# A four-layer network on one core: the scan's product with B queued ahead of other VectorE steps, and small matmuls in column quarters

## The chip, the cores and the metric

One core of one Trainium2 chip. The metric is device time in microseconds (us) of one launch. Engines: PE (TensorE), PEld (its weight loads), DVE (VectorE), ACT (ScalarE), POOL (GpSimd), SP (SyncE, which issues DMAs).

## The reference

Four images x of 96 channels by 64 x 64 pixels go through four layers, each with a residual.

```
x = x + ssm(group_norm(x))          # layer 0: norm, projection, 3x3 conv, selective scans in
                                    # 4 directions, norm, gate z, projection
x = x + deform(group_norm(x))       # layer 1: offsets, mask = 3x3 conv; bilinear samples; conv
t = tokens(x)
t = t + fft_mix(layer_norm(t)); t = t + ffn_fp8(layer_norm(t))          # layer 2
t = t + linear_attn(layer_norm(t)); t = t + ffn_fp8(layer_norm(t))      # layer 3
```

The selective scan, for each of 4 images, 4 directions, 192 channels d and 16 states n, over 4096 positions:

```
h[t] = exp(delta[t] * A[d,n]) * h[t-1] + (delta[t] * u[t]) * B[n,t]
y[t] = sum over n of h[t] * C[n,t]
```

A layer norm needs, at each position, the mean over channels of the squared centred values (the variance).

## The kernel before, in words

**The scan.** Layer 0's scan is cut into 1536 units (`Unit`): 8 channels x 16 states on the 128 partitions, 1024 positions in a row. A unit passes five engines. `fetch` (ACT's DMA queue) brings delta, copied to all states, as `da`; `decay` (L895, ACT) makes exp(delta A) of it; `inflow` (L901, PE) spreads delta u over the partitions into `db`, a PSUM tile with two buffers; `recur` multiplies db by B in place (L915, DVE) and runs the recurrence over da and db (L918, DVE) into `hh`; `weigh` (L925, L927, POOL) multiplies hh by C; `total` (L946, PE) folds the states of two units into `py`, with 32 output columns a product, in four column groups of the array; `settle` and `store` bring the sum out. B and C come with `fetch_step`, delta u with `fetch_block` on SP's queue, six units ahead for `fetch_block`.

`scan` writes out the order by hand. In iteration n it issues, if due, `fetch_step` and `fetch_block`, then inflow(n+1), decay(n+2), total(n-5, n-4) in odd iterations, one fetch, recur(n) with product and recurrence together, weigh(n-2), settle, store, and yields.

**Everything else** runs beside it in two streams of Python generators, joined in `layers23`: `ends` (layer 0's `before` for images 0 to 3, then layers 2 and 3 of each image) and `middle` (`behind`, layer 0's output norm and projection, and layer 1 of each image). An image can be sampled only when its scans are done, and layers 2 and 3 of an image wait for its layer 1. After each unit, the streams put in steps until the planner says stop. Nothing waits at run time for the plan: the plan fixes the order of each engine's instructions, and `in_program_order` keeps it.

**The planner.** `Clock` keeps for each engine the planned end of what is queued. A step names its work as costs in us (`cost(pe=.., dve=..)`); `has_room` lets it in if each engine it uses is planned to end no later than now plus AHEAD (3, 3, 5, 7 us). "Now" is VectorE's planned end or `due`, whichever is later, and `due` grows by PACE (4.8 us) a unit. BESIDE (6 us) bounds the VectorE work beside one unit. `pipe` runs the chains of one stage, a few at a time; tags in `takes` and `frees` count buffers. Outside pipelines (group norm statistics, the steps of `inv_sqrt_steps`, `positions`) a step goes through `Stream.step` alone.

**Norm.** `centred` does one layer norm's first part, in 8 chunks of 512 positions: a product with the centring matrix (L457, PE, "lnc"), square and copy (L462, L463, ACT), and a product of the squares with a matrix whose only non-zero column is number j (L468, PE, "lnv"), so that chunk j's variance lands in row j of one accumulator. Then 1/sqrt, and `spread` (L483) brings row j back to all partitions with a one-hot column of the identity. It is called in `normed_rows` (layer 0) and `normed` (layers 2 and 3). `behind` has its own such norm over 192 channels (L1022, "va"), two chunks at a time.

**Offsets.** `offsets` (layer 1) convolves the padded image with 27 filters, padded to 96 columns: 9 products a chunk, all into the same PSUM rows (L1149, "po"). ScalarE adds the bias (L1159, "oc"), PE transposes the pixels (L1165, "pt") and the offsets (L1170, "pm"), ScalarE copies both, and SP issues 8 stores of the pixels per chunk into a table in DRAM (L1178), from which the samples are gathered (L1251, POOL's queue). Samples are weighted at L1260 (DVE) and transposed at L1277 (PE). The other VectorE step named below is L752 (softplus in layer 0's `steps`).

Of the kernel before, what the change touches and what calls it, by code (L numbers as in the profile page):

```python
# [25 lines left out]
CH = 512  # L26
# [18 lines left out]
def prepare(x, **w):  # L45
# [66 lines left out]
    a["wom"] = wide(om.transpose(1, 2, 0), 96)  # L112
# [87 lines left out]
PACE = 4.8  # L200


class Clock:
# [4 lines left out]
    def __init__(self):  # L208
        self.ends = [0.0] * 4

        self.own = 0.0


        self.idle, self.beside = 0.0, 0.0

        self.due = 0.0

# [8 lines left out]
    def has_room(self, work, ready):  # L226
        now = self.now()
        idle = self.idle if self.own is None else self.own
        if self.own is None and work[DVE] and self.beside >= BESIDE:
            return False  # L230
        first = next((e for e in (PE, ACT, DVE, POOL) if work[e]), None)
        if ready > (now if first is None else max(self.ends[first], idle)):
            return False
        return all(not w or e <= now + a for w, e, a in zip(work, self.ends, AHEAD))

# [25 lines left out]
def pipe(net, chains, width, every=0, **tiles):  # L261
# [5 lines left out]
    while True:  # L267
# [9 lines left out]
        for n, chain in enumerate(active):  # L277
# [4 lines left out]
            if not all(free[tag] for tag in chain.takes):  # L282
                continue
# [5 lines left out]
        for tag in chain.takes:  # L289
            free[tag] -= 1  # L290
        step = next(chain.steps, None)
# [41 lines left out]
class Net:  # L333
# [3 lines left out]
    def __init__(self, ctx, tc, ins):  # L337
# [5 lines left out]
        for name in ("vecs", "ident", "cen96", "grp3"):  # L343
# [3 lines left out]
        for n in (C, DI):  # L347
            t = self.to_row[n] = self.const.tile([128, 135], F32, name=f"to_row{n}")
            nc.vector.memset(t, 0.0)
            nc.vector.memset(t[:, 7:8], 1.0 / n)  # L350
# [96 lines left out]
    def centred(self, x, cen, dst, key, pool, bias=None):  # L447
# [4 lines left out]
        self.hold(1)  # L452

        def chain(j):
            cs = slice(j * CH, (j + 1) * CH)
# [3 lines left out]
            sq = pool.tile([C, CH], F32, name=f"lnq{key}_{j}", tag="lnq", bufs=2)  # L459
# [4 lines left out]
            else:  # L464
                nc.scalar.activation(sq, pc, AF.Square, bias=bias)
                nc.scalar.activation(d, view(pc), AF.Identity, bias=bias)
            yield cost(pe=1.1, act=1.2)
            nc.tensor.matmul(  # L468
                var, lhsT=self.to_row[C][:C, 7 - j : 135 - j], rhs=sq, start=(j == 0), stop=(j == NCH - 1)
            )  # L470
            yield cost(pe=1.0)

        yield from pipe(self, (chain(j) for j in range(NCH)), 2)
# [36 lines left out]
class Layer0:  # L510
# [95 lines left out]
    def normed_rows(self, b, x, pad, rows, as_rows):  # L606
# [3 lines left out]
        with tc.tile_pool(name=f"l0n{b}", bufs=2) as sm:  # L610
# [21 lines left out]
            def chain(j):  # L632
                pb = net.spread(rs, j, C, f"0_{b}")
# [152 lines left out]
    def scan(self):  # L786
# [23 lines left out]
        for n in range(len(units) + 7):  # L810
# [3 lines left out]
            if n == 0:  # L814
# [5 lines left out]
                self.inflow(at(0))  # L820

# [20 lines left out]
            clock.unit(self.scanned[1])  # L842
            yield True

# [64 lines left out]

    def recur(self, u, free):  # L910

        nc, clock = self.net.nc, self.net.clock
        clock.add(DVE, 1.22, u.spread)
        self.scanned = (self.scanned[1], clock.add(DVE, 2.33, max(u.decayed, free)))
        nc.vector.tensor_mul(u.db, u.db, u.bc[:, 0, :])  # L915
# [52 lines left out]
    def behind(self, b):  # L968
# [6 lines left out]
        with (  # L975
# [4 lines left out]
            for j0 in range(NCH - HB, -1, -HB):  # L980
# [18 lines left out]
                def centred(i):  # L999
# [12 lines left out]
                    for g, (o, c0, n) in enumerate(((ca, 0, 128), (cc, 128, D2))):  # L1012
# [24 lines left out]
                def gated(i):  # L1037
# [6 lines left out]
                    pb = net.spread(rstd, i, 128, key)  # L1044
# [26 lines left out]
class Layer1:  # L1071
# [41 lines left out]
    def offsets(self, b, om):  # L1113
# [3 lines left out]
        with tc.tile_pool(name=f"l1a{b}", bufs=1, side="right") as pre:  # L1117
# [26 lines left out]
            def chunk(j):  # L1144
                r0 = j * NR
                po = net.mm(f"po{b}_{j}", 96)
                for k in range(9):
                    dy, dx = divmod(k, 3)
                    nc.tensor.matmul(  # L1149
                        po,  # L1150
                        lhsT=wom[:, k, :],
                        rhs=pad[:, r0 + dy : r0 + dy + NR, dx : dx + W],
                        start=(k == 0),
                        stop=(k == 8),
                    )
# [13 lines left out]
                for q in range(4):  # L1169
                    nc.tensor.transpose(pm[:, q, :], oc[:, 128 * q : 128 * q + 128], net.ident[:27, :27])  # L1170
# [293 lines left out]
def normed(net, t, tl, key, pool):  # L1464
# [6 lines left out]
    def chain(j):  # L1471
        cs = slice(j * CH, (j + 1) * CH)
        pb = net.spread(rs, j, C, key)
# [251 lines left out]
```

## Time and profile before

| | us |
|---|---|
| median of three runs | 9105.8 (9103.93 to 9124.99) |
| the profiled execution | 9119.14 |
| its span, first to last instruction | 9117.0 |
| first scan starts / last scan ends | 368.2 / 7990.6 |
| VectorE busy / GpSimd / PE / ScalarE | 6993.7 / 6374.1 / 6752.4 / 4179.8 |
| mean granted PE clock | 0.818 of full speed |

A row of instructions in the profile reads: line, engine, operation, names out<-in, shape, count, then busy time in us and mean ns of one, then the engine's idle time just before them and what ended most of it. A row of the timeline reads: start, duration (us), engine, line, operation, names, shapes, count of merged instructions, and in brackets the idle time before with its releaser. An fp32 matmul shows as two records. The page's slices, a fortieth of the span each (tenths of busy time):

```profile
DVE  0367877887898898878898989889899988836514
POOL 0486679766789998787799977666799966627701
PEclk8676977798777899777888987789888878886597
```

The dense stretches of POOL (slices 12 to 15, 20 to 22, 29 to 31) are the gathers of images 0, 1 and 2; those of image 3 lie in slices 36 and 37, after the scan.

### The profile page before, as it was taken

The page shows a single profiled execution, that of the slowest core. Times are in us where ns is not written, and L with a number is a line of the kernel's source. Part 1 is how long each engine was busy: PE and PEld are TensorE (multiplying, and loading weights), DVE is VectorE, ACT ScalarE, POOL GpSimd, SP SyncE. Part 2 cuts the span into 40 slices and gives each one's busy share as a digit, 9 for nine tenths or more (in the row PEclk, how much of TensorE's full clock was granted, in tenths as well). Part 3 has the DMA queues.
Part 4 walks back from the last instruction along what each step waited for, and adds up shares of the span by engine and source line. Part 5 has one row for each costly group of instructions (what it writes and reads, how often), then busy time and mean ns, then how long its engine had stood idle before and what let it go on. Part 6 is the DMA issues. An engine that isn't in the chain of part 4 may idle for free.

```text
span 9117.0 us, 93017 instructions
## 1 busy us (share of the span) xinstructions
PE 6752.4 (74%) x31832; PEld 3066.5 (34%) x31832; DVE 6993.7 (77%) x4932; ACT 4179.8 (46%) x5798; POOL 6374.1 (70%) x4755
## 2 busy tenths in 40 slices
PE   6664967697866679676788877788777768885497
PEld 2111311132222234211245542244433435433283
DVE  0367877887898898878898989889899988836514
ACT  4574667565554445566533335543343344431123
POOL 0486679766789998787799977666799966627701
PEclk8676977798777899777888987789888878886597
DMA  1466777777877887787888876677777777824410
GB/s 50 127 184 170 186 194 213 202 185 180 210 208 210 218 211 207 201 210 192 213 209 218 212 189 173 172 189 188 210 197 197 197 166 190 190 59 139 130 52 12
DMA packets 775821, 1609.05 MB, mean 176 GB/s; under 512 B 247665, under 2 KB 338829, under 8 KB 773238
## 3 DMA queue, kind: packets, MB, share of 16 engines
q10 hardware_dynamic: 244224, 843.17, 36.7%
q1 hardware_dynamic: 457398, 533.38, 21.7%
q0 software_dynamic: 73728, 226.57, 9.3%
q8 instruction: 253, 4.15, 0.2%
q14 instruction: 218, 1.79, 0.1%
HBM read 1346.50 MB, written 256.29 MB: 176 GB/s over the span
## 4 chain that ended last, share of the span: by engine, by line
PE 34%; DVE 21%; POOL 16%; DMA 13%; issue 9%; ACT 5%; SPq 1%; ACTq 0%; DVEq 0%; POOLq 0%
DVE hh L918 9%; POOL hh L927 7%; DVE db L915 5%; PE pc L662 5%; POOL g L1251 4%; PE py L946 4%; PE f L1371 3%; PE db L901 3%; PE ps L1277 3%; PE po L1149 2%; DVE g L1260 2%; DMA da<-de 2%; DMA du<-du 2%; PE pd L1293 2%; DMA g<-table,idx 1%
## 5 line engine op out<-in xcount | busy, mean ns | idle before, releaser
L927 POOL TENSOR_TENSOR hh<-hh,bc 128x1024 f32<-128x1024 f32 x1536 | 3665.5, 2388 | 350.0 <-DVE hh L918 234.6
L918 DVE TENSOR_TENSOR_SCAN hh<-da,st,db 128x1024 f32<-128x1024 f32 x1152 | 2703.5, 2347 | 217.0 <-PE py L946 67.3
L915 DVE TENSOR_TENSOR db<-db,bc 128x1024 f32<-128x1024 f32 x1536 | 1868.7, 1217 | 409.8 <-PE db L901 398.1
L895 ACT ACTIVATE da<-da,w_al 128x1024 f32<-128x1024 f32 x1536 | 1742.4, 1148 | 742.0 <-DMA da<-de 300.5
L901 PE MATMUL db<-du,rep 96*128 96x512 bf16 x3072 | 1072.3, 437 | 802.5 <-DVE hh L918 733.0
L1251 POOL DMA_INDIRECT g<-table,idx x1152 | 1340.3, 1163 | 397.7 <-issue 230.8
L946 PE MATMUL py<-hh,w_fold 128*32 128x512 f32 x6144 | 1094.7, 734 | 103.3 <-POOL hh L927 77.6
L918 DVE TENSOR_TENSOR_SCAN hh<-da,db 128x1024 f32<-128x1024 f32 x384 | 877.9, 2286 | 62.1 <-PE py L946 8.8
L1277 PE MATMUL ps<-w_ident,g 128*96 128x128 f32 x3744 | 603.3, 320 | 385.7 <-issue 250.1
L901 PEld LDWEIGHTS <-rep 96*128 96x128 bf16 x3072 | 275.2, 105 | 1736.2 <-issue 1153.0
L1260 DVE TENSOR_TENSOR g<-g,wt 128x1152 f32<-128x1152 f32 x384 | 701.8, 1828 | 163.9 <-DMA g<-table,idx 158.7
L1285 ACT COPY st<-ps 96x384 f32<-96x384 f32 x384 | 182.0, 474 | 1233.0 <-PE ps L1277 1085.0
L925 POOL COPY st<-hh 128x1 f32<-128x1 f32 x1152 | 280.3, 243 | 654.7 <-DVE hh L918 601.9
L1277 PEld LDWEIGHTS ps<-w_ident,g 128*96 128x96 f32 x3744 | 493.7, 148 | 616.6 <-issue 369.2
L749 POOL TENSOR_TENSOR w<-w,ex 128x512 f32<-128x512 f32 x192 | 245.7, 1280 | 525.4 <-ACT w L746 519.4
L662 PE MATMUL pc<-pad,wc 96*128 96x512 f32 x1152 | 533.6, 610 | 45.7 <-DMA wc<-wc_d 42.1
L752 DVE SCALAR_TENSOR_TENSOR rl<-pd,lw 128x512 f32<-128x512 f32 x192 | 130.9, 682 | 475.0 <-POOL lw L750 461.2
L771 PE MATMUL pr<-ex,w_ident 128*128 128x512 f32 x384 | 287.2, 838 | 158.8 <-POOL ex L761 79.5
L946 PEld LDWEIGHTS py<-hh,w_fold 128*32 128x32 f32 x6144 | 162.7, 120 | 633.2 <-issue 391.2
L1517 POOL CAST xqf<-fl 96x512 fp8e5<-96x512 f32 x64 | 46.8, 738 | 454.5 <-DVE fl L1475 407.4
L662 PEld LDWEIGHTS pc<-pad,wc 96*128 96x128 f32 x1152 | 219.1, 195 | 325.1 <-issue 309.7
L1293 PE MATMUL pd<-st,wdc 96*128 96x256 f32 x1152 | 315.1, 426 | 4.2 <-ACT st L1285 3.1
(249 smaller groups left out, 9519.0 us busy)
## 6 DMA issues: line engine op xcount, KB each, us to landing
da<-de ACTq DMA_DIRECT2D x1536, 512.0 KB
du<-du SPq DMA_DIRECT2D x512, 192.0 KB
bc<-bcd SPq DMA_DIRECT2D x128, 512.0 KB
du<-du SPq DMA_DIRECT2D x128, 384.0 KB
y<-yb SPq DMA_DIRECT2D x384, 128.0 KB
de<-rl SPq DMA_DIRECT2D x128, 256.0 KB
m<-in_dft SPq DMA_DIRECT2D x128, 256.0 KB
ad<-y ACTq DMA_DIRECT2D x192, 128.0 KB
```

Of the source, the lines that this page charges most:

```text
L662: nc.tensor.matmul(pp, lhsT=wc[:, q, g * 128 : (g + 1) * 128], rhs=pad[:, r0 + dy : r0 + dy + NR, dx : dx + W], start=(q == 0), stop=(q == 8),
L771: nc.tensor.matmul(pr, lhsT=net.ident, rhs=ex, start=True, stop=False)
L895: self.net.nc.scalar.activation(u.da, u.da, AF.Exp, scale=self.al[:, a : a + 1])
L901: self.net.nc.tensor.matmul(db[:, h, :], lhsT=self.rep[:96, u.s % 4, :], rhs=u.du[u.s // 4][:, h * CH : (h + 1) * CH], start=True, stop=True,)
L915: nc.vector.tensor_mul(u.db, u.db, u.bc[:, 0, :])
L918: nc.vector.tensor_tensor_scan(u.along(u.hh), u.along(u.da), u.along(u.db), first, ALU.mult, ALU.add)
L927: self.net.nc.gpsimd.tensor_mul(u.hh, u.hh, u.bc[:, 1, :])
L946: nc.tensor.matmul(py[p0 : p0 + 32], lhsT=self.fold[:, u.i, :], rhs=hc[:, h * CH : (h + 1) * CH], start=u.sums["add"] is None and u.i == 0 ...
L1251: nc.gpsimd.indirect_dma_start(out=g[:, k, :], out_offset=None, in_=self.tables[b % 2], in_offset=bass.IndirectOffsetOnAxis(ap=idx[:, n : ...
L1260: nc.vector.tensor_mul(g4, g4, w4.unsqueeze(2).to_broadcast([128, 12, C]))
L1277: nc.tensor.matmul(pt[:, k, :], lhsT=g[:, k, c * C : (c + 1) * C], rhs=net.ident, is_transpose=True, start=(c == 0), stop=(c == corners - 1),)
L1293: nc.tensor.matmul(po, lhsT=wdc[:, k, :], rhs=st[:, k, :], start=(k == 0), stop=(k == 8))
```

## The change

1. The product of unit n+1 with B leaves `recur` for a method of its own, `enter`. After unit n has been issued it is pending. `pipe` calls `precede` ahead of each step it issues: if that step has VectorE work and db of unit n+1 is planned to be there MARGIN (0.5 us) before VectorE's planned end, the product is issued ahead of the step. What is still pending when the streams are done is issued then, ahead of the next unit.
2. PACE goes from 4.8 to 4.7.
3. The offsets' convolution writes product k to rows 32 (k mod 4) onward, with filters padded to 32 columns; the bias is added over all 128 rows (only rows 0 to 26 have one), and the transposes of the offsets become products with a matrix `add4`, which sums the four quarters on the way.
4. The variances: a chunk writes its own quarter of the columns (32 wide), and four chunks' products are issued together in a chain `sums`; square buffers go from two to four and are counted by a tag. Chunk j's variance lands in row 32 (j mod 4) + j div 4. In `behind` the two chunks write halves (64 columns).

```diff
-    a["wom"] = wide(om.transpose(1, 2, 0), 96)
+    a["wom"] = wide(om.transpose(1, 2, 0), 32)
+    a["add4"] = (np.arange(128)[:, None] % 32 == np.arange(27)[None]).astype(f)
...
-PACE = 4.8
+MARGIN = 0.5
+PACE = 4.7
...
+    def precede(self, work):
+        if self.enter and work[DVE] and self.own is None and self.entered + MARGIN <= self.ends[DVE]:
+            self.enter()
...
@@ pipe
-            if not all(free[tag] for tag in chain.takes):
+            if not all(free[tag] > 0 for tag in chain.takes):
...
+        clock.precede(known.get((chain.kind, chain.done), (0.0,) * 4))
         step = next(chain.steps, None)
...
@@ Net.__init__
-            t = self.to_row[n] = self.const.tile([128, 135], F32, name=f"to_row{n}")
+            t = self.to_row[n] = self.const.tile([128, 65], F32, name=f"to_row{n}")
...
-            nc.vector.memset(t[:, 7:8], 1.0 / n)
+            nc.vector.memset(t[:, 1:2], 1.0 / n)
...
@@ Net.centred
+            yield wait(new=True, takes="sq")
...
-            sq = pool.tile([C, CH], F32, name=f"lnq{key}_{j}", tag="lnq", bufs=2)
+            sq = sqs[j] = pool.tile([C, CH], F32, name=f"lnq{key}_{j}", tag="lnq", bufs=4)
...
-            yield cost(pe=1.1, act=1.2)
-            nc.tensor.matmul(
-                var, lhsT=self.to_row[C][:C, 7 - j : 135 - j], rhs=sq, start=(j == 0), stop=(j == NCH - 1)
-            )
-            yield cost(pe=1.0)
-
-        yield from pipe(self, (chain(j) for j in range(NCH)), 2)
+            yield cost(pe=1.1, act=1.2, frees=f"v{j // 4}")
+
+        def sums(r):
+            yield wait(takes=f"v{r}")
+            for q in range(4):
+                nc.tensor.matmul(
+                    var[32 * q : 32 * q + 32],
+                    lhsT=self.to_row[C][:C, 1 - r : 33 - r],
+                    rhs=sqs[4 * r + q],
+                    start=(r == 0),
+                    stop=(r == 1),
+                )
+            yield cost(pe=1.3, frees="sq sq sq sq")
+
+        def chains():
+            for r in range(2):
+                for q in range(4):
+                    yield chain(4 * r + q)
+                yield sums(r)
+
+        yield from pipe(self, chains(), 5, every=-99, sq=4, v0=-3, v1=-3)
...
@@ normed_rows and normed
-                pb = net.spread(rs, j, C, f"0_{b}")
+                pb = net.spread(rs, 32 * (j % 4) + j // 4, C, f"0_{b}")
...
@@ scan: before the first unit, and after each unit
+                self.next = at(0)
+                self.enter()
...
+            self.next = at(n + 1)
+            if self.next is not None:
+                clock.enter, clock.entered = self.enter, self.next.spread
             yield True
+            if clock.enter:
+                self.enter()
...
+    def enter(self):
+        u, clock = self.next, self.net.clock
+        clock.enter = None
+        clock.add(DVE, 1.22, u.spread)
+        self.net.nc.vector.tensor_mul(u.db, u.db, u.bc[:, 0, :])
+
     def recur(self, u, free):
         nc, clock = self.net.nc, self.net.clock
-        clock.add(DVE, 1.22, u.spread)
         self.scanned = (self.scanned[1], clock.add(DVE, 2.33, max(u.decayed, free)))
-        nc.vector.tensor_mul(u.db, u.db, u.bc[:, 0, :])
...
@@ behind
-                            var,
-                            lhsT=net.to_row[DI][:n, 7 - i : 135 - i],
+                            var[64 * i : 64 * i + 64],
+                            lhsT=net.to_row[DI][:n, 1:65],
                             rhs=sq,
-                            start=(i == 0 and g == 0),
-                            stop=(i == HB - 1 and g == 1),
+                            start=(g == 0),
+                            stop=(g == 1),
...
@@ offsets
-                po = net.mm(f"po{b}_{j}", 96)
+                po = net.mm(f"po{b}_{j}")
                 for k in range(9):
                     dy, dx = divmod(k, 3)
+                    p0 = 32 * (k % 4)
                     nc.tensor.matmul(
-                        po,
+                        po[p0 : p0 + 32],
...
-                        start=(k == 0),
-                        stop=(k == 8),
+                        start=(k < 4),
+                        stop=(k >= 5),
                     )
-                    if k in (2, 5):
-                        yield cost(pe=2.6, holds=1, takes="oc" if k == 5 else "")
-                oc = pre.tile([27, CH], F32, name=f"oc{b}_{j}", tag="oc")
-                nc.scalar.activation(oc, po[:27], AF.Identity, bias=net.vec(V_OMB, 27))
-                yield cost(pe=2.6, act=0.7, new=True, takes="pix")
+                yield cost(pe=3.0, holds=1, takes="oc")
+                oc = pre.tile([128, CH], F32, name=f"oc{b}_{j}", tag="oc")
+                nc.scalar.activation(oc, po, AF.Identity, bias=net.vec(V_OMB))
+                yield cost(act=0.7, new=True, takes="pix")
...
-                    nc.tensor.transpose(pm[:, q, :], oc[:, 128 * q : 128 * q + 128], net.ident[:27, :27])
+                    nc.tensor.matmul(
+                        pm[:, q, :], lhsT=oc[:, 128 * q : 128 * q + 128], rhs=net.add4, start=True, stop=True
+                    )
```

More of the change, by code (lines that the diff above doesn't have):

```diff
@@ L216, in __init__ @@
         self.due = 0.0
+        self.enter, self.entered = None, 0.0
     def now(self):
@@ L342, in __init__ @@
         self.psum = ctx.enter_context(tc.tile_pool(name="mm", bufs=3, space=PSUM))
-        for name in ("vecs", "ident", "cen96", "grp3"):
+        for name in ("vecs", "ident", "cen96", "grp3", "add4"):
             setattr(self, name, self.load(name, self.const))
@@ L452, in centred @@
         self.hold(1)
+        sqs = {}
         def chain(j):
+            yield wait(new=True, takes="sq")
             cs = slice(j * CH, (j + 1) * CH)
@@ L1043, in gated @@
                     nc.sync.dma_start(zc, self.z_d[b][128:, cs])
-                    pb = net.spread(rstd, i, 128, key)
+                    pb = net.spread(rstd, 64 * i, 128, key)
                     yield cost(pe=1.2, holds=1)
@@ L1472, in chain @@
         cs = slice(j * CH, (j + 1) * CH)
-        pb = net.spread(rs, j, C, key)
+        pb = net.spread(rs, 32 * (j % 4) + j // 4, C, key)
         yield cost(pe=1.2, holds=1)
```

## The prediction

> **What bounds the kernel now.** I read the stage sums first, then the groups, then single stretches of the timeline.
>
> The stretch sums (columns: window, length, then busy time and instructions of PE, PEld, DVE, ACT, POOL, then clock, DMA share, GB/s), cut at the first and the last scan:
>
> ```profile
> 0.00:368.00 368.00, 224.99 (x452) 87.51 (x453) 25.80 (x52) 163.81 (x203) 39.11 (x38) 0.79 0.23 64
> 368.00:7991.00 7623.00, 5738.65 (x27140) 2483.21 (x27140) 6489.29 (x4229) 3733.61 (x5028) 5899.10 (x4342) 0.83 0.76 196
> 7991.00:9117.00 1126.00, 788.80 (x4241) 495.82 (x4240) 478.58 (x652) 282.36 (x567) 435.93 (x376) 0.77 0.29 79
> ```
>
> The scan stage is 7623 of 9117 us, and VectorE is its fullest engine: 6489/7623 = 85%, POOL 77%, PE 75%. The groups show what VectorE does there (busy, mean ns | idle before, releaser):
>
> ```profile
> L918 DVE TENSOR_TENSOR_SCAN hh<-da,st,db 128x1024 f32<-128x1024 f32 x1152 | 2703.5, 2347 | 217.0 <-PE py L946 67.3
> L915 DVE TENSOR_TENSOR db<-db,bc 128x1024 f32<-128x1024 f32 x1536 | 1868.7, 1217 | 409.8 <-PE db L901 398.1
> L1260 DVE TENSOR_TENSOR g<-g,wt 128x1152 f32<-128x1152 f32 x384 | 701.8, 1828 | 163.9 <-DMA g<-table,idx 158.7
> L752 DVE SCALAR_TENSOR_TENSOR rl<-pd,lw 128x512 f32<-128x512 f32 x192 | 130.9, 682 | 475.0 <-POOL lw L750 461.2
> ```
>
> Now VectorE's timeline (start, duration):
>
> ```profile
> 4010.31 2.35 DVE L918 TENSOR_TENSOR_SCAN hh<-da,st,db 128x1024 f32<-128x1024 f32 x1
> 4012.57 0.67 DVE L752 SCALAR_TENSOR_TENSOR rl<-pd,lw 128x512 f32<-128x512 f32 x1
> 4013.16 1.22 DVE L915 TENSOR_TENSOR db<-db,bc 128x1024 f32<-128x1024 f32 x1
> 4014.51 2.35 DVE L918 TENSOR_TENSOR_SCAN hh<-da,st,db 128x1024 f32<-128x1024 f32 x1
> 4016.78 1.21 DVE L915 TENSOR_TENSOR db<-db,bc 128x1024 f32<-128x1024 f32 x1
> ```
>
> See two things. Instructions that don't need each other start 0.08 us before the recorded end of the one ahead (4012.57+0.67 = 13.24, next at 13.16). The scan, which needs the product just ahead of it, starts 0.13 us after that ends (4013.16+1.22 = 14.38, scan at 14.51). So the product directly ahead of its scan costs 0.21 us more than any other neighbour would. And the side step (L752 here) stands ahead of the product, so if it waits, the product waits with it. I counted the whole timeline: between 667 of the 1535 pairs of scans there is at least one side step, 868 have none (3.57 us a unit).
>
> After the scans one image is left. Its offsets are bound by PE, its table stores are the next thing:
>
> ```profile
> 8121.29 0.49 PE L1165 MATMUL pt<-w_ident,x 96*128 96x96 f32 x4
> 8121.72 0.42 PE L1170 MATMUL pm<-w_ident,oc 27*128 27x27 f32 x4
> 8122.07 7.97 PE L1149 MATMUL po<-pad,w_wom 96*96 96x512 f32 x18
> L1178 SPq DMA_DIRECT2D table<-pix x64: 574/622/632, 8113.7 to 8176.7; - x64
> ```
>
> A chunk comes every 8.58 us (8122.07, 8130.65), all of it PE; an fp32 product is two records, so nine products are x18, 0.88 us each. The last line (min/median/max ns of one issue) says that a chunk's eight stores hold SP for about 8 x 0.66 = 5.3 us; they start 0.66 us apart.
>
> **What the Trainium skill says.** (1) "TensorE: Matmul & The Clock Gate", Measured speedup vs the span model: matmuls to different column groups run together, three of M=32, N=512 in 1/2.38 of the time. The trace agrees: eight records of the fold (L946, 32 columns each, four products) take 1.07 us at full clock, where four full products take 4 x 0.86; about 3.2 times. (2) "TensorEngine Tiling (Array Packing)", PSUM Bottleneck: behind a 4x faster TensorE something else becomes the bound. Here ScalarE's 1.4 us a chunk does not, SP's 5.3 does. (3) "SBUF — State Buffer", Who interferes with whom: a VectorE instruction with two SBUF inputs contends with GpSimd, one with a single SBUF input doesn't. The trace agrees: L915 and L918, each with db in PSUM, keep 1.22 and 2.35 us, L1260 takes from 1.33 to 3.5. Moving the product thus brings no new contention. (4) "VectorE: DVE Perf Modes", The DRAIN you can't avoid: a semaphore between chained operations costs nothing extra. Here a dependent pair costs 0.21 us more than an independent one; the measurement decides.
>
> **The change part by part.** The sum is made against the profiled execution, 9119.1 us (span 9117.0), 13.3 above the median 9105.8.
>
> *Product ahead.* Removes and adds no instruction, and no DMA moves; on VectorE's queue alone product n+1 passes the side steps of unit n (fetches, decay and inflow are on other queues). Gain 1: where a side step lies between product and scan, the 0.21 us are covered: 667 x 0.21 = 139 us. Gain 2: idle time ahead of side steps is 461 us, 373 of it ahead of a unit's first one; product n+1 can run in that time if its db is there. Cost: the product now meets db earlier. Queued behind the waiting product are the side steps of unit n, and behind those PE's transposes and ScalarE's copies. In 127 of the 667 units db ended after the scan ahead. I re-timed each of the 667 units with every input's arrival held as traced: product first, then the side steps, then the scan. Sum: 261 us gained, 66 lost, net 194. The guard MARGIN leaves the product back where the plan has db late, which takes from the loss (without those units the gain is 243). Against it, side results leave VectorE 1.14 us later, and PE, POOL and ScalarE wait for them. Bounds: +243 gained, and a loss as in rival D. I take 80% of gain 1 (111; in gather stages POOL is also 90% busy) and a third of the other 55 (18): **-129 us**. Steps outside the pipelines (norm statistics, positions) don't call the guard and keep their place.
>
> *PACE 4.7.* The plan leaves 0.1 us less a unit for side work. Side steps' VectorE time is 1216 us, the plan's room 1536 x (4.7-3.55) = 1766, so nothing has to fall out; only in the last image's 384 units may 38 us slip behind the scan. Cover: layers 2 and 3 of image 2 end at 8544, gathers of image 3 at 8629, so 85 us hide it. Without it +38; with sparser side work perhaps -38. I take 0.
>
> *Offsets in quarters.* 288 products. Per chunk 4+4+1 in column groups: 1.07+0.86+0.86 = 2.8 us for 7.9. The four transposes of oc become fp32 products with 27 columns; the trace has none such: 0.42 us as now, or 4 x 0.28 = 1.1 at the price of L1437's (0.141 a record). Even at 1.1, PE needs 2.8+0.5+1.1 = 4.4 us, under SP's 5.3, so SP hides it. The bias on 128 rows in place of 27 costs the same 0.68 us, one element column per step. Image 3: 8 x (8.58-5.33) = 26 us, nothing ahead but PE: **-25**. Images 0 to 2 (110 us each, at 4.0 us a unit, VectorE's pace): 0, since VectorE idles 5 to 13 us in each; bound -31. Their stores come closer together on SP: two chunks' sixteen hold it for 10.6 us, and the scan's du loads queue behind them; those are issued six units (24 us) ahead of their use, which covers it, else up to 10 us an image.
>
> *Variances in quarters.* 160 products of 172 us become 40 groups of about 1.1, saving 128 us of PE. Inside the scan stage PE is not the bound: 0. A norm after it: lnc from 8653.5 to the last lnv at 8671.0, 17.4 us, PE-bound. After: 0.94 for the first lnc, four pairs of ScalarE steps at 0.97, the group 1.1, then again (the four squares' buffers are free only after the first group): about 12. Four norms of image 3 and one at the start: 5 x 5 = 25; I take **-20**, since only image 3's are surely alone on their chain. The layer-0 output norm in halves: its two products never lie side by side, 0. The extra load of add4 is one small DMA among some at the start: 0, bound +2.
>
> Sum: -129 -25 -20 = -174: 9119 - 174 = 8945, less 13 for the median: about **8930**.
>
> **Rivals.** *A, forecast:* as summed, 8930, own range 8870 to 9010. *B, all of the re-timing holds* and the freed PE helps the scan stage: -243 -31 -45 -13 from 9119 = 8787 at the very most; with 194 and half of the 31, 8850. For it: gain 1 is arithmetic. Against: POOL at 90% in gather stages. *C, the scan stage gains nothing,* the waits only change places: 9119-45-13 = 9061, from 9040 to 9110. For it: 398 us of VectorE's idle is already the product waiting for db. *D, slower:* PE's queue is in order, and steps that wait for a side result stand ahead of the next db. Twelve transposes of a gather (12 x 0.161 = 1.93 us) and db (0.70) make 2.6, with hand-overs 2.9, while the scan that now alone covers them lasts 2.35: 0.5 us of new waiting a unit. In all 667 units: 334 lost in place of 194 gained at 0: 334 - 194 + (-45): +95, 9119+95-13 = 9200. It decides from (194+45)/667 = 0.36 us a unit. Against it: only 279 of the 667 units hold an L1260, and the guard. That the product is not moved, because the guard refuses it, is C.
>
> **Numbers.** A 0.55, B 0.18, C 0.13, D 0.14. About 0.3% (27 us) is what a measurement of this kernel can tell from no change: 9078 to 9133. Faster: A, B, half of C and a little: 0.78; same: most of the other half of C and the edge of D, 0.08; slower 0.14. The range 8840 to 9130 leaves out D and the end of B.
>
> **What would show it.** Scans starting 0.08 us before the recorded end of a side step; idle before L918 down from 279 us by some 80; idle before L752 and L1260 down; last scan at about 7860; chunks of offsets after it every 5.3 us, stores back to back on SP; a norm's first part about 12 us. Wrong would be: idle before L915 (398 on db) up by over 150 us, or the last scan not before 7960.

## The result, and the profile after

After the change the median is 9148.0 us (9136.2 to 9153.0, four runs), beside 9104.9 (9087.2 to 9125.0) for the kernel before on the same chip: ratio 1.0045, 95% interval 1.0022 to 1.0068. The kernel became slower by 0.45%; the forecast was 8930. The profiled execution took 9148.4 us, its span is 9146.0, that is 29 above the 9117.0 of before.

The stretch sums of the kernel after (window, length, busy time and instructions of PE, PEld, DVE, ACT, POOL, then clock, DMA share, GB/s), cut at its first and last scan:

```profile
0.00:372.50 372.50, 222.63 (x452) 85.00 (x453) 25.80 (x52) 163.21 (x203) 39.16 (x38) 0.79 0.22 65
372.50:8058.80 7686.30, 5673.29 (x27088) 2422.70 (x27087) 6444.79 (x4220) 3724.38 (x5012) 5902.11 (x4341) 0.81 0.76 194
8058.80:9146.00 1087.20, 762.59 (x4422) 485.44 (x4420) 489.50 (x660) 288.45 (x583) 438.25 (x376) 0.77 0.30 83
```

The start is 4 us longer, the scan stage 64 longer (7622 to 7686), what follows the last scan (the tail) 39 shorter (1126 to 1087): 4 + 64 - 39 = 29. In the scan stage VectorE is busy 44 us less (6489.2 to 6444.8), and idle 108 us more. The groups show where the idle time is:

```profile
L960 DVE TENSOR_TENSOR_SCAN hh<-da,st,db 128x1024 f32<-128x1024 f32 x1152 | 2700.0, 2344 | 207.8 <-PE py L988 73.4
L952 DVE TENSOR_TENSOR db<-db,bc 128x1024 f32<-128x1024 f32 x1536 | 1863.9, 1213 | 573.5 <-PE db L938 562.5
L1305 DVE TENSOR_TENSOR g<-g,wt 128x1152 f32<-128x1152 f32 x384 | 688.0, 1795 | 204.6 <-DMA g<-table,idx 196.9
L782 DVE SCALAR_TENSOR_TENSOR rl<-pd,lw 128x512 f32<-128x512 f32 x192 | 131.3, 684 | 443.3 <-POOL lw L780 429.7
```

L952 is the product (L915 before), L960 the scan (L918). The product's wait for db rose from 398 to 562 us, which is the sign that the prediction named as "wrong" (over 150), and the last scan ends at 8058.8, not before 7960. The idle time before the scans, which was to fall by some 80 us, fell by 6 (279.1 to 272.6, both forms of the scan together): the small gaps of dependent pairs shrank, other waits grew. The waits of VectorE within the scan stage (us in total, times, longest), before:

```profile
DVE db L915 <- PE db L901: 376.6, 189, 26.8
DVE rl L752 <- POOL lw L750: 189.5, 87, 14.1
DVE hh L918 <- PE py L946: 76.1, 64, 13.3
DVE g L1260 <- DMA g<-table,idx: 68.9, 39, 7.1
```

and after:

```profile
DVE db L952 <- PE db L938: 536.5, 233, 17.1
DVE rl L782 <- POOL lw L780: 156.0, 76, 11.5
DVE g L1305 <- DMA g<-table,idx: 97.5, 35, 10.6
DVE hh L960 <- PE py L988: 89.5, 86, 6.7
```

The waits for db grew by 160 us, those for gathers (L1305, L1260 before) by 29, while those of L782 (L752 before) fell by 33. Yet the move did what it says. VectorE's timeline of the kernel after (start, duration):

```profile
3913.44 1.21 DVE L952 TENSOR_TENSOR db<-db,bc 128x1024 f32<-128x1024 f32 x1
3914.56 0.68 DVE L1105 TENSOR_TENSOR xr<-po,xr 96x512 f32<-96x512 f32 x1
3915.15 2.33 DVE L960 TENSOR_TENSOR_SCAN hh<-da,st,db 128x1024 f32<-128x1024 f32 x1
```

The side step lies between product and scan, and the scan starts 0.09 us before its recorded end (3914.56 + 0.68 = 3915.24). Counted over the timeline: the product stands ahead of all side steps in 291 units, between them in 77, and behind them in 245, where the guard, or a step that does not call it, left it.

### The profile page after: what moved, and what is told of

The parts are those of the page before. It is cut to its first block, busy times and chain, and to the rows that moved or that the text cites. A ratio compares the mean times of both kernels' runs of the same rounds, so it can differ in the third digit from the quotient of the medians.

```text
span 9146.0 us, 93251 instructions
## 1 busy us (share of the span) xinstructions
PE 6658.5 (73%) x31960; PEld 2993.1 (33%) x31960; DVE 6960.1 (76%) x4932; ACT 4176.0 (46%) x5798; POOL 6379.5 (70%) x4755
## 4 chain that ended last, share of the span: by engine, by line
PE 31%; POOL 20%; DVE 18%; DMA 14%; issue 10%; ACT 6%; SPq 1%; ACTq 1%; DVEq 0%; POOLq 0%
POOL hh L969 9%; DVE hh L960 8%; POOL g L1296 7%; DVE db L952 4%; PE pc L692 4%; PE py L988 3%; PE f L1416 3%; PE db L938 3%; DMA da<-de 2%; PE ps L1322 2%; DMA du<-du 2%; DMA g<-table,idx 2%; PE pd L1338 1%; DVE g L1305 1%; POOL lw L780 1%
## 5 line engine op out<-in xcount | busy, mean ns | idle before, releaser
L960 DVE TENSOR_TENSOR_SCAN hh<-da,st,db 128x1024 f32<-128x1024 f32 x1152 | 2700.0, 2344 | 207.8 <-PE py L988 73.4
L952 DVE TENSOR_TENSOR db<-db,bc 128x1024 f32<-128x1024 f32 x1536 | 1863.9, 1213 | 573.5 <-PE db L938 562.5
L988 PE MATMUL py<-hh,w_fold 128*32 128x512 f32 x6144 | 1140.7, 746 | 146.8 <-POOL hh L969 130.0
L960 DVE TENSOR_TENSOR_SCAN hh<-da,db 128x1024 f32<-128x1024 f32 x384 | 876.9, 2284 | 64.8 <-PE py L988 16.1
L1305 DVE TENSOR_TENSOR g<-g,wt 128x1152 f32<-128x1152 f32 x384 | 688.0, 1795 | 204.6 <-DMA g<-table,idx 196.9
L782 DVE SCALAR_TENSOR_TENSOR rl<-pd,lw 128x512 f32<-128x512 f32 x192 | 131.3, 684 | 443.3 <-POOL lw L780 429.7
```

The source lines that it names most:

```text
L952: self.net.nc.vector.tensor_mul(u.db, u.db, u.bc[:, 0, :])
L960: nc.vector.tensor_tensor_scan(u.along(u.hh), u.along(u.da), u.along(u.db), first, ALU.mult, ALU.add)
L988: nc.tensor.matmul(py[p0 : p0 + 32], lhsT=self.fold[:, u.i, :], rhs=hc[:, h * CH : (h + 1) * CH], start=u.sums["add"] is None and u.i == 0 ...
L1305: nc.vector.tensor_mul(g4, g4, w4.unsqueeze(2).to_broadcast([128, 12, C]))
```

## The experiments

Each ran beside the kernel before on the same chip. "db" is VectorE's wait for db in the scan stage, by the trace. Scan stage, tail and db are in us from one profiled execution each; the ratio is of the medians, with its 95% interval.

| run | edit | ratio | scan stage | tail | db |
|---|---|---|---|---|---|
| before | | 1 | 7622 | 1126 | 377 |
| after | all | 1.0045 (1.0022 to 1.0068) | 7686 | 1087 | 537 |
| e1 | product ahead | 1.0133 (1.0107 to 1.0159) | 7689 | 1156 | 536 |
| e9, 4.79 | e1, PACE 4.79 | 1.0118 (1.0103 to 1.0134) | 7655 | 1179 | 507 |
| e9, 4.81 | e1, PACE 4.81 | 1.0110 (1.0093 to 1.0126) | 7653 | 1205 | 458 |
| e4 | product ahead, plan kept | 1.0011 (1.0001 to 1.0021) | 7630 | 1116 | 490 |
| e5 | booking alone | 1.0083 (1.0066 to 1.0101) | 7672 | 1152 | 398 |
| e2 | PACE 4.7 | 0.9996 (0.9981 to 1.0010) | 7571 | 1172 | 370 |
| e6 | PACE 4.79 | 0.9998 (0.9986 to 1.0011) | 7562 | 1170 | 368 |
| e7 | PACE 4.81 | 0.9968 (0.9955 to 0.9980) | 7589 | 1128 | 367 |
| e3 | offsets and variances | 1.0067 (1.0047 to 1.0087) | 7691 | 1109 | 459 |
| e10, 4.79 | e3, PACE 4.79 | 1.0056 (1.0041 to 1.0072) | 7684 | 1100 | 491 |
| e10, 4.81 | e3, PACE 4.81 | 1.0101 (1.0083 to 1.0118) | 7698 | 1100 | 454 |
| e12 | variances alone | 0.9984 (0.9975 to 0.9993) | 7619 | 1093 | 399 |
| e11 | offsets alone | 1.0055 (1.0035 to 1.0075) | 7720 | 1068 | 434 |
| e8 | offsets alone, old steps and costs | 0.9962 (0.9944 to 0.9980) | 7624 | 1099 | 391 |
| e16 | offsets alone, old steps, low costs | 1.0090 (1.0075 to 1.0106) | 7763 | 1071 | 520 |
| e15 | e8, PACE 4.81 | 0.9943 (0.9929 to 0.9958) | 7596 | 1082 | 376 |
| e13 | after, PE's AHEAD 1.8 | 1.0001 (0.9987 to 1.0015) | 7559 | 1167 | 426 |
| e14 | before, PE's AHEAD 1.8 | 1.0011 (1.0001 to 1.0022) | 7543 | 1216 | 347 |

**One part alone: e1, e2, e3.** e1 is part 1 of the change on the kernel before; e2 and e3 are

```diff
 e2, on before
-PACE = 4.8
+PACE = 4.7
 e3, on after
-PACE = 4.7
+PACE = 4.8
-        clock.precede(known.get((chain.kind, chain.done), (0.0,) * 4))
```

> Before, with part 1 of the change alone (product ahead, its 1.22 us booked at once), PACE 4.8, no quarters. Theory order: slower than before by 60 us or more, like the order-only kernel. Theory plan: slower than the order-only kernel by 80 us or more, since booking the product early moves VectorE's planned end, and with it the planner's now, and so every side step behind it. Theory pace or quarters: faster than before by 80 us or more.

> Before, with PACE 4.7 alone. My prediction: no change (within 38 us either way), with the end of image 2's layers 3 some 40 us nearer to the end of image 3's gathers. Theory pace (the sparser plan is what costs): slower by 60 us or more, in the scan stage. Theories order and plan: within 40 us.

> Before, with parts 3 and 4 alone (offsets and variances in quarters or halves), PACE 4.8, the product in its old place. My prediction: 45 us faster, all of it outside the scan stage: offsets of the last image in about 43 us for 68, each norm's first part in about 12 us for 17. Theory quarters (changed costs in the plan, or bursts on PE and SP, cost the scan stage): scan stage longer by 50 us or more, so no gain in all.

Measured beside 9099.6 us: the product ahead costs 1.33% (9218.6), PACE nothing (9099.9), the quarters cost 0.67% (9165.8). The three make 2.0% by themselves and 0.45% together, so they are not additive. Both edits that were to save time lose it in the scan stage (+67 and +69 us), and e1 loses 29 more in the tail. One changes no instruction's length, and the other makes PE's work shorter, so the first suspects are the order of the instructions and the plan that sets it. A lower clock is a rival: the scan stage's granted PE clock is 0.83 before and 0.81 to 0.82 in the kernels that lost. But it is 0.81 in e8, e13 and e15 too, with scan stages of 7624, 7559 and 7596 us, so it does not by itself cost the time.

**Order or plan: e4 and e5.** In e4 the product moves as in e1, but its 1.22 us are booked where they were, so the plan is that of before: the other engines have the same instructions in the same order, and only VectorE's order differs (373 of the 667 products that have a side step ahead of them moved). In e5 the booking moves and the product stays in `recur`.

```diff
 e4, on e1: in enter
-        clock.add(DVE, 1.22, u.spread)
 in recur
+        clock.add(DVE, 1.22, u.spread)
 e5, on e1: in enter
-        self.net.nc.vector.tensor_mul(u.db, u.db, u.bc[:, 0, :])
 in recur
+        nc.vector.tensor_mul(u.db, u.db, u.bc[:, 0, :])
```

> Before, with the product queued ahead under the same guard, but the planner still books its 1.22 us where it did (in recur). So every other instruction keeps its place on every engine; only 373 products move ahead of side steps on VectorE. Theory order (the move itself costs, because the product now waits for db): slower than before by 60 us or more, idle ahead of the product up by over 100 us. Theory plan (the move itself gains what the re-timing said, and the loss comes from side steps being laid out anew): faster by 80 to 190 us, first of all the 373 x 0.21 = 78 us of the dependent pair.

> The complement of the order-only kernel: the planner books the product's 1.22 us ahead of the side steps under the same guard, but the product is issued in its old place, right ahead of its scan. All engines but VectorE then have the order of the kernel with part 1 alone, which was 1.3% slower. Theory plan (the loss comes from side steps laid out anew): slower than before by 80 us or more, scan stage about 7690 us. Theory order (the product's new place on VectorE costs, but only in that plan): within 30 us of before.

e4 took 9112.6 beside 9099.6 us (+0.11%): the move by itself gains nothing. e5 took 9188.8 beside 9098.3 (+0.83%): most of e1's loss comes with the new plan, in the profiled run 49 us in the scan stage and 26 in the tail. The rest of e1's loss, 1.33% against 0.83%, appears when the product is moved within that plan. In e5's scan stage the wait for db is not what grew most, since it rose by 21 us and the wait for gathers by 38:

```profile
DVE db L938 <- PE db L919: 397.9, 197, 17.5
DVE g L1283 <- DMA g<-table,idx: 107.1, 47, 8.1
```

VectorE's waits in e4's scan stage:

```profile
DVE db L932 <- PE db L919: 489.7, 237, 32.8
DVE rl L763 <- POOL lw L761: 170.7, 79, 14.2
DVE g L1283 <- DMA g<-table,idx: 59.7, 25, 6.4
```

Against before: db +113, L763 -19, L1283 -9. The gaps of under 0.25 us ahead of a scan sum to 141 us, 46 less than before (187), and VectorE's busy time fell by 33 (6489 to 6456), since a scan now overlaps the side step ahead of it by some 0.08 us. 46 + 33 = 79 us is just what 373 moved products at 0.21 us promise (78). So the gain is there, and the waits for db take it back: -46 - 33 + 113 - 19 - 9 = +6, beside a scan stage that is 8 us longer. PE is at work during 392 of the 490 us of these waits, on db itself or on what stands ahead of it. How that happens in one unit, in VectorE's timeline of e4 (start, duration; in brackets the idle time before):

```profile
6812.71 2.35 DVE L941 TENSOR_TENSOR_SCAN hh<-da,st,db 128x1024 f32<-128x1024 f32 x1
6817.73 1.23 DVE L932 TENSOR_TENSOR db<-db,bc 128x1024 f32<-128x1024 f32 x1 [2.67 <-PE db L919]
6818.87 2.20 DVE L1283 TENSOR_TENSOR g<-g,wt 128x1152 f32<-128x1152 f32 x1
6820.99 2.33 DVE L941 TENSOR_TENSOR_SCAN hh<-da,st,db 128x1024 f32<-128x1024 f32 x1
```

and PE's at the same time:

```profile
6811.73 1.92 PE L969 MATMUL py<-hh,w_fold 128*32 128x512 f32 x4 [1.55 <-POOL hh L950]
6813.58 2.74 PE L1300 MATMUL ps<-w_ident,g 128*96 128x128 f32 x12
6816.15 1.10 PE L1545 MATMUL phf<-xqf,w1q 96*128 96x512 fp8e5 x3
6817.10 1.02 PE L919 MATMUL db<-du,rep 96*128 96x512 bf16 x4
```

The next db stands in PE's queue behind a fold, twelve transposes of samples and an fp8 product; PE is busy from 6811.73 on and reaches db 4.4 us after the scan began (at 6812.71). In the kernel before, the same unit has the same PE instructions, and db comes 4.4 us after the scan too (scan 6801.88, db 6806.30). But there VectorE filled that wait:

```profile
6801.88 2.35 DVE L918 TENSOR_TENSOR_SCAN hh<-da,st,db 128x1024 f32<-128x1024 f32 x1
6804.56 1.36 DVE L1260 TENSOR_TENSOR g<-g,wt 128x1152 f32<-128x1152 f32 x1 [0.33 <-DMA g<-table,idx]
6807.16 1.23 DVE L915 TENSOR_TENSOR db<-db,bc 128x1024 f32<-128x1024 f32 x1 [1.24 <-PE db L901]
6808.52 2.35 DVE L918 TENSOR_TENSOR_SCAN hh<-da,st,db 128x1024 f32<-128x1024 f32 x1
```

From scan to scan it is 6.64 us before and 8.28 in e4: 0.84 of the difference is a slower L1283 (2.20 us for 1.36; why is not shown, and over the whole scan stage these instructions took only 8 us more), the other 0.80 is wait for db that the side step no longer fills, since it follows it.

**Is a new plan only luck? e6, e7, e9, e10.** Any change of a number in the plan can change the order of many instructions, so PACE was moved by 0.01 in the kernel before (e6, e7), in e1 (e9) and in e3 (e10).

```diff
 e6, e7 on before; e9 on e1; e10 on e3
-PACE = 4.8
+PACE = 4.79   (the other of each pair: 4.81)
```

> A change of no weight: PACE 4.79 in place of 4.80 in the kernel before. It moves about as many instructions to other places as part 1 did. Theory scatter (any new layout of the side steps changes the scan stage by some tens of us, up or down): off by 20 us or more in the scan stage or the tail, sign open. Theory systematic (part 1 and the quarters cost for a reason of their own): within 15 us in the scan stage.

> The same on the other side, PACE 4.81. Theory scatter: scan stage off by 20 us or more, not in proportion to the 0.01. Theory systematic: within 15 us.

> Part 1 alone (product ahead and booked at once) with PACE 4.79. The kernel before took 7562 to 7622 us for its scan stage at 4.79, 4.80 and 4.81, the kernel with part 1 took 7689 at 4.80. Theory systematic (booking the product early lays out side steps in a way that costs): scan stage above 7650 again, time 60 us or more over before. Theory scatter: scan stage anywhere from 7560 to 7690, and its mean over 4.79, 4.80, 4.81 within 40 us of before's mean of 7591.

> Part 1 alone with PACE 4.81. As for 4.79: systematic says above 7650 and 60 us or more over before; scatter says that it may lie anywhere from 7560 to 7690.

> Offsets and variances in quarters (parts 3 and 4) with PACE 4.79, product in its old place. At 4.80 the scan stage was 7691 us, 69 over before. Theory systematic (the quarters' new costs and the norm's new chain cost the scan stage): above 7650 again, 20 us or more over before in time. Theory scatter: from 7560 to 7690; then with the 28 us that quartered offsets save after the scan, the time is below before's.

> The same with PACE 4.81: systematic says a scan stage above 7650, scatter says that it may lie anywhere from 7560 to 7690.

Luck has a size: with nothing else changed, the scan stage goes from 7622 to 7562 and 7589, the tail from 1126 to 1170 and 1128, and the time by 0.3% at most. The losses are larger and stay. Mean ratio over PACE 4.79, 4.80 and 4.81: 0.9989 for the kernel before, 1.0120 with the product ahead, 1.0075 with the quarters; mean scan stage 7591, 7666 and 7691 us. The three scan stages of the kernel before (7562 to 7622) do not overlap those with the product ahead (7653 to 7689) or with the quarters (7684 to 7698). So luck of this size explains neither loss. But the kernel before had the slowest scan stage of its three, and a difference of 0.3% that comes with a new plan is not to be read as an effect; the 0.45% of the whole change, measured at a single PACE, is only a little more. Neither part was run alone at the whole change's PACE of 4.7.

**Offsets or variances: e8, e11, e12, e16, e15.** e12 and e11 are e3 with the offsets, or the norms, as before. e8 has e11's instructions with the planner's old three steps of 2.6 us a chunk. e16 keeps three steps but books 1.0 us for each. e15 is e8 with PACE 4.81.

```diff
 e8, on e11: after products 2 and 5, and with the bias
-                yield cost(pe=3.0, holds=1, takes="oc")
+                    if k in (2, 5):
+                        yield cost(pe=2.6, holds=1, takes="oc" if k == 5 else "")
...
-                yield cost(act=0.7, new=True, takes="pix")
+                yield cost(pe=2.6, act=0.7, new=True, takes="pix")
 e16, on e8, each of the three
-                        yield cost(pe=2.6, holds=1, takes="oc" if k == 5 else "")
+                        yield cost(pe=1.0, holds=1, takes="oc" if k == 5 else "")
...
-                yield cost(pe=2.6, act=0.7, new=True, takes="pix")
+                yield cost(pe=1.0, act=0.7, new=True, takes="pix")
 e15, on e8
-PACE = 4.8
+PACE = 4.81
```

> Offsets in quarters, but with the steps and costs of before, so that the planner lays everything out as before; only the instructions of the convolution itself are different. Theory plan: scan stage within 15 us of before, the gathers of the last image 15 to 25 us earlier after the last scan (stores bound by SP), 10 to 25 us faster in all. Theory quarters (the concurrent products themselves disturb the scans): scan stage longer by 30 us or more.

> Offsets in quarters with their new steps and costs (one step of 3.0 us on PE for three of 2.6), norms as before, PACE 4.8. If the offsets' step is what lengthens the scan stage: wait of the product for db above 440 us (before about 370), scan stage above 7650, time at or over before. If not: like the kernel with old steps and costs, 20 to 30 us faster.

> Variances in quarters and halves alone, offsets as before, PACE 4.8. If the norms' new chain is what lengthens the scan stage (four products at once in one step, five chains wide): wait for db above 440 us, scan stage above 7650, 20 us or more over before. If not: up to 15 us faster, from four norms that are 3 us shorter each after the scan.

> The quartered offset products with the chunk's three steps kept, but each step's planned PE cost 1.0 us in place of 2.6; PACE 4.8. Tells why the offsets with one step of 3.0 us and then none lengthened the scan stage by 98 us (7720) where the same instructions under the costs of before did not (7624). If it is the cheap planned cost, which lets the chunks and so the 64 stores come earlier and closer together in the scan stage: scan stage about 7700 and the time 0.4% or more above before. If it is the single long step put ahead of db in PE's queue: scan stage within 40 of 7620 and the time 0.2 to 0.5% below before, as with the old costs. If it is scatter of the layout, a value between them.

> The quartered offset products with the three steps and planned costs of before, and PACE 4.81. The two by themselves measured 0.38% and 0.32% below before, the first in the tail (28 us), the second in the scan stage (33 us). If the planner's layout were smooth in its numbers the two would add to 0.7%: about 9042 us. If a new PACE scatters the layout, as other PACE values did (30 us in the scan stage, 25 in the tail), anything from 9020 to 9100. Slower than before would speak against a real gain of the quartered products.

The variances gain a little (0.16%, within the bound of no change). The quartered offsets gain 0.38% in e8, in the profiled runs all of it in the tail (1126 to 1099). As e8 books the costs of before, VectorE, ScalarE and GpSimd run their instructions in exactly the order of before, so no luck of a plan is in this gain. In e11 they lose 0.55%: same products, other costs. e16 tells the two differences between them apart: three short steps with low costs lose as well (0.90%), so it is not the one long step that is needed for the loss, and the low cost is what e11 and e16 have in common. (With the old costs the ratios are 0.9962 and 0.9943, with low ones 1.0055 to 1.0101 in five runs: more apart than luck.) The new costs are the true ones (a chunk's PE work is 2.77 + 0.55 + 1.00 = 4.3 us in the timeline below, booked at 3.0 + 1.2; e8 books 9.0). The old ones, now twice too high, perhaps kept room on PE's queue; that is a reading, not a measurement of the queue. VectorE's wait for db in e8's scan stage:

```profile
DVE db L916 <- PE db L902: 390.6, 185, 25.6
```

and in e16's:

```profile
DVE db L916 <- PE db L902: 520.4, 210, 26.7
```

The wait for db grew by 130 us, of a scan stage that is 139 longer. In e11 it is a smaller part: 43 us more than e8's, of a scan stage 96 longer. (The positions' first step, whose load is queued on SP behind the chunks' 64 stores, is a small item: 30 us of waits in e8, 41 in e16.) By units, e16 falls behind e8 by 31 us between scans 432 and 480, 34 between 816 and 864, and 62 between 1200 and 1248, that is where an image's offsets end and its gathers begin; a part is given back later. It also loses 33 between 1056 and 1104, where no offsets run.

e15 is faster than the kernel before and the whole change: 9046.7 us beside 9097.7, ratio 0.9943. Against before, its tail is 44 us shorter and its scan stage 26, and the latter is of the size that PACE 4.81 alone gave by luck (33 in e7):

```profile
368.70:7964.70 7596.00, 5656.28 (x26884) 2431.95 (x26883) 6479.34 (x4220) 3728.49 (x5006) 5892.48 (x4341) 0.81 0.76 197
7964.70:9046.90 1082.20, 765.91 (x4632) 493.40 (x4624) 490.69 (x660) 295.58 (x590) 434.43 (x376) 0.81 0.29 83
```

**PE's depth: e13 and e14.** If it is PE's queue filled ahead of db, less planned work ahead on PE should help the changed kernel more than the kernel before.

```diff
 e13 on after, e14 on before
-AHEAD = (3.0, 3.0, 5.0, 7.0)
+AHEAD = (1.8, 3.0, 5.0, 7.0)
```

> The changed kernel with PE's part of AHEAD at 1.8 us in place of 3.0, so that fewer side steps stand in PE's queue ahead of the next db. Theory PE queue: wait of the product for db down from 540 us to about 400 or less, scan stage shorter by 60 us or more than the changed kernel's 7686; side work slips behind the scan, so the tail grows. Rival (the wait has another origin, such as single long steps): wait for db still above 480 us.

> Control: the kernel before with PE's part of AHEAD at 1.8. Theory PE queue: its wait for db falls too, but by less (from about 370 us by 30 to 80), as its product has the side steps of the unit to cover db; scan stage shorter by up to 40 us, tail longer.

The changed kernel goes from 1.0045 to 1.0001, its scan stage from 7686 to 7559 and its wait for db to

```profile
DVE db L952 <- PE db L938: 425.7, 203, 23.1
```

that is -111 us; in the kernel before the same edit takes 30 us off that wait and 79 off the scan stage, and adds 89 to the tail (1216), so that the time stays (1.0011). The difference, 111 - 30 = 81 us, is about half of the 160 that the change added to that wait. It points to the depth of PE's queue, but does not prove it: 426 us lies between what the theory (400) and its rival (over 480) expected, and with the product ahead PACE alone moved this wait by 78 us (458 to 536 in e1 and e9). Nor does it make the change a gain: side work that is put off in the scan stage is found again after it (tail 1167 against 1087).

## Why the prediction was wrong, point by point

**The bound.** That VectorE is the fullest engine of the scan stage is right; that its time could be cut by 129 us by reordering its own queue is not. 398 us of waits for db were on the page, and rival C read them rightly: VectorE's pace also hangs on when db comes through PE's queue, behind the side products there.

**Product ahead, -129: the step that failed.** It was the re-timing "with every input's arrival held as traced". Its first gain was real: 0.21 us at each moved product, 79 us in e4 for 373 of them (294 of the 667, 44%, stayed where they were; the prediction took 20% off). But what was to be saved is spent on waiting: e4, with nothing else changed, waited 113 us more for db. The product meets db earlier, the side step that used to fill the wait stands behind it, and so does what other engines need from that step. Held arrivals allowed 66 us of loss and a net of 194 us gained; measured, the scan stage is 8 us longer. This is the mechanism of rival D, at 113/373 = 0.30 us a moved product in place of 0.5 on all 667. By itself it gives rival C's time, no change.

**The plan, not costed at all.** The prediction let the edit move one instruction. Booking 1.22 us earlier changes what `has_room` lets in: in e1 and e5 the instructions of PE, VectorE, ScalarE and GpSimd run in another order than before. That alone was +0.83% (e5). No rival held it. The measured 9148 lies between the times of C and D, but is neither's sum: the order by itself gave C's time, and the plans' losses came on top.

**PACE 4.7, 0: right in sum, not shown in its reason.** In e2 the scan stage became 51 us shorter and the tail 45 longer. The cover of 85 us was used up: image 2's layers 2 and 3 ended 554 us after the last scan before, and 712 in e2, after the last gather's issue (618). But a tenth of the step (e6, PACE 4.79) did the same: scan stage -60, tail +43. So neither shift can be put down to the 0.1 us, and that they cancel in the time is luck.

**Offsets, -25.** The terms were right. PE's timeline of the kernel after, in the tail (x counts records):

```profile
8150.76 2.77 PE L1193 MATMUL po<-pad,w_wom 96*32 96x512 f32 x18
8153.46 0.55 PE L1208 MATMUL pt<-w_ident,x 96*128 96x96 f32 x4
8153.85 1.00 PE L1213 MATMUL pm<-w_add,oc 128*128 128x27 f32 x8
8154.78 2.77 PE L1193 MATMUL po<-pad,w_wom 96*32 96x512 f32 x18
```

2.77 us for the nine products, where 2.8 were estimated from the fold, 1.00 for the four products with add4, where 1.1 was the upper bound. The Trainium skill's "TensorEngine Tiling (Array Packing)", PSUM Bottleneck, names the copies out of PSUM as what may become the bound behind a faster TensorE; here it was not ScalarE's copies but the stores on SP, whose queue shows the eight chunks' stores as one run:

```profile
8150.54 45.41 SPq L1223 DMA_DIRECT2D table<-pix  x64
```

45.4 us where they took 63.6 (8113.7 to 8177.3). From the start of the offsets to the start of the gathers it is 90 us before, and 64.5 in e8: there the forecast 25 came true. In the kernel after it is 83, so only 7 were kept, as from the last store to the first gather it took 30 us in place of 15: VectorE ran image 2's last steps between those that make the sampling positions. "Images 0 to 2: 0" failed: by the plan, not by the products (e8: scan stage +2, e11: +98).

**Variances, -20.** PE's timeline of one norm of image 3:

```profile
8695.68 7.02 PE L472 MATMUL lnc<-t,w_cen 96*128 96x512 f32 x8 [11.38 <-DMA t<-x]
8702.63 1.80 PE L488 MATMUL lnv<-lnq,to_row 96*32 96x512 f32 x8
8704.36 3.70 PE L472 MATMUL lnc<-t,w_cen 96*128 96x512 f32 x8
8707.99 2.20 PE L488 MATMUL lnv<-lnq,to_row 96*32 96x512 f32 x8
```

14.5 us in place of 17.4; 12 were forecast. This norm saves 2.9 us where 5 were taken, mostly because a group of four takes 1.8 to 2.2 and not 1.1 (the spans can hold waits for the squares). Four such norms would make 12; the start did not gain (first scan at 372.5 against 368.2).

**The tail in all**: -39 where -45 was forecast, though partly by a shift of side work. The scan stage: +64 where -129 was forecast. That one term makes 193 of the 203 us by which the profiled execution (9148) missed its sum (8945).

**Two slips of the working.** 667 x 0.21 is 140, not 139. L1260 was said to take from 1.33 to 3.5 us; over the trace of before it takes from 1.29 to 8.18, with a median of 1.36 and ten of the 384 above 3.5. Neither changes the sum by more than an us.

**What stays open.** Why the plan with the early booking, or with true costs of the offsets, lays the side work worse: the runs show that it does (for the product ahead and for the quarters over three values of PACE), and where most of the offsets' loss comes, but no single decision of the planner was isolated. The planner's code suggests one reading: "now" is VectorE's planned end, so booking the product early moves it 1.22 us on, and with it the limit up to which each engine may be filled, as if AHEAD were 1.22 us larger. e13 takes 1.2 us off PE's AHEAD, but was run on the whole change only; e1 or e5 with that AHEAD would test the reading, and that e5's wait for db rose by only 21 us speaks against a large share of PE in it. Nor is it shown why the parts are not additive, 2.0% by themselves and 0.45% together.

## What to carry to other kernels

Where the fullest engine already waits for another one's product, moving that product's use earlier in its queue may only move the waiting; a re-timing that holds arrivals fixed does not give the gain (here 194 us by the re-timing, none measured), so first ask what stands ahead of the producer in its own in-order queue. In a kernel whose order comes from planned costs, a change of a cost or of the time at which it is booked can change the whole order: price it by a run in which only the booking changes, measure the scatter with changes that mean nothing, and don't change a cost in the same step as the instructions. A cheaper instruction is worth what its own stage gives, which is read where nothing else runs beside it (here the tail).

## What of the hardware was not expected

Nine fp32 products of 32 columns in four column groups took 2.77 us, where nine in one group of 96 took 7.97, which is 2.9 times as long. Products with a 128-row, 27-column moving operand cost 1.00 us for four (eight records), the transposes that they replace 0.42. On VectorE, two instructions that don't depend on each other overlapped by some 0.08 us, and a dependent pair had a gap of 0.13; over 373 moved products that is 30 and 48 us, and e4 recovered 33 us of busy time and 46 of gaps.
